# Two more products in seven steps: gate_w's second and w3's second product of the first group, with sums made by way of a PSUM bank

## The chip, the cores and the metric

The kernel runs on one NeuronCore of a Trainium2 chip. The metric is the device time of one launch in microseconds. Engines are named as the profile names them: PE is the matrix engine (PEld its weight loads), DVE the vector engine, ACT the scalar engine, POOL the GpSimd engine, SP the engine whose queue issues nearly all DMAs.

## What is computed

Inputs are 4,096 tokens of width 1,024, all in fp32. Cut to what matters, with the constants of the layers left out:

```python
xn = layernorm(u)                                  # 4096 x 1024
g = sigmoid(xn @ gate_w.T + gate_b); u_g = xn * g  # only its mean over time and 8 rows per block are used
s = c * scan(b * u_g) + (d + d_lr(mean(u_g))) * u_g
h1 = silu(xn @ w1.T)
h2 = silu(h1 @ w3.T)
h3 = h2 @ w2.T
out = scatter_add(gates * h3, top-2 of softmax(xn @ wr.T))   # into 8 rows
x = u + s * silu(out)
```

The scatter adds into the rows 0 to 7 alone, since the indices are those of the eight experts. Everything else of the output is a copy of u. The work is the product with gate_w (needed for 1,024 tokens), with w1 and w3 (needed for all tokens), and the routing.

## The kernel before, in words

The tokens are taken in four groups of 1,024 (`NS` = 4, `sb` 0 to 3). In each group there is a product `u` (xn with w1) and a product `m` (h1 with w3); group 0 has a product `g` (xn with gate_w) too. Each of these 1024 x 1024 x 1024 products is done by a scheme of the Strassen kind on two levels. The outer level has seven products of half size, numbered 1 to 7, of sums of the left blocks and sums of the weight blocks. The class `Half` (line 859) does one of them. Inside it, a second level of the same scheme makes seven steps of a half-size product instead of eight; a `plain` half has eight steps and needs no inner sums. A step (`small`, line 843) is four matmuls of 128x128 by 128x256.

An inner product needs four sums of each operand. `left_sums` (line 822) makes those of the left block and `fresh_sums` (line 559) those of a weight block, both on POOL, a quarter of a block (128x512) at a time, into tiles named `q`; `keep` also writes the weight sums to DRAM for the later groups. Where a half of group 0 is plain, `late_sums` (line 612) makes and keeps w3's sums at the beginning of group 1. Every partial result goes from PSUM to SBUF by an ACT copy or a DVE add (`first`, `more`): four times in a plain half, seven times in one with seven steps.

The outer sums of the left blocks are `s1` to `s4` (lines 777 to 820), each of four pieces of 128x512, on DVE in group 0. The outer sums of the weights are in `first_weights` (w1 and gate_w) and `first_w3` (`take`). Some of them go `with_bank` (line 599): ACT copies one operand to a PSUM bank and DVE takes the sum with that bank as its second operand. The banks are the accumulator `acc` (number 0), which is idle until the first scatter, and a bank `spare` (number 1). The gate's sigmoid (`gated`, line 1033) uses the same two.

The order of the work is written out. `line` lists the halves, `start` gives each a place; a half's steps stand two places apart, so two halves alternate, and one place is one step of PE. `at(place, f)` puts a piece of work at a place, and a generator's `yield n` puts its rest n places later. Each engine gets its instructions in the order that results, and keeps to it. The order within group 0 is u and g in turn (1, 2, 5, 6, 7, 4, 3), then m (1, 5, 6, 2, 7, 4, 3). `norm` (line 421) normalizes the next group's tokens during m: it loads rows of means and scales from DRAM, ACT copies them to the bank `spare`, and DVE subtracts and multiplies. Blocks (20), quarters (18) and the two X banks of PSUM are handed on in turn.

Of the kernel before, what the change touches and what calls it, by code (L numbers as in the profile page):

```python
# [14 lines left out]
ALU = mybir.AluOpType  # L15
# [7 lines left out]
def kernel(  # L23
# [162 lines left out]
    def at(place, f, *args):  # L186

        seq[0] += 1
        heapq.heappush(todo, (place, seq[0], f, args))
# [14 lines left out]

    order = {"u": (1, 2, 5, 6, 7, 4, 3), "m": (1, 5, 6, 2, 7, 4, 3)}
    line = []
    PLAIN_M = (2, 7)
    PLAIN_G = (1, 2)
    for i in order["u"]:
        line += [("u", 0, i, i == 1), ("g", 0, i, i in PLAIN_G)]  # L210
    line += [("m", 0, i, i in PLAIN_M) for i in order["m"]]
# [209 lines left out]
    def norm(sb, bcs):  # L421

        flat = bcs[sb].rearrange("(o s i t) p -> o s i (t p)", o=1, s=2, i=4)
        held = {}

        def load(n):
            held[n] = quarter()
            sync.dma_start(
                held[n].tile.rearrange("p (s n) -> p s n", s=2),
                flat[:, :, n, :].to_broadcast([P, 2, Q]),  # L430
            )

        load(0)
        for I in range(2):
            for a in range(2):
                n = 2 * I + a
                if n < 3:
                    load(n + 1)
                yield 1.5
                bc = ps_acc.tile([P, 2, Q], F32, tag="rows", name=f"bc_{sb}{n}")  # L440
                act.copy(bc.rearrange("p s n -> p (s n)"), held[n].tile)
                held[n].drop()
                for J in range(2):
                    p = part(xn[sb, I, J], a)
                    for s, op in ((0, ALU.add), (1, ALU.mult)):
                        yield norm_step[sb]
                        row = bc[:, s : s + 1, :].to_broadcast([P, 4, Q])
                        dve.tensor_tensor(p, p, row, op)

    norm_step = {1: 1.6, 2: 1.9, 3: 1.9}  # L450

    def route(sb):

# [123 lines left out]
    def sub(eng, out, p, q, n=4, step=0.5):  # L577

        for h in range(0, 4, 4 // n):
            eng.tensor_tensor(  # L580
                out[:, h : h + 4 // n], p[:, h : h + 4 // n], q[:, h : h + 4 // n], ALU.subtract
            )
            yield step

    free_banks = [0, 1]

    def spare_bank():


        while not free_banks:  # L590
            yield 0.25
        taken[0] = free_banks.pop(0)

    taken = [0]

    def bank_tile(n):
        return acc if n == 0 else ps_acc.tile([P, H], F32, tag="rows", name="spare")

    def with_bank(out, p, q, order=(0, 1, 2, 3), swap=False):


        for j in order:
            yield from spare_bank()
            n = taken[0]
            ps = bank_tile(n)
            act.copy(ps, q[:, j])
            yield 0.5
            a, b = (ps, p[:, j]) if swap else (p[:, j], ps)
            dve.tensor_tensor(out[:, j], a, b, ALU.subtract)
            free_banks.append(n)  # L610

    def late_sums(name, i):

# [100 lines left out]
    def first_w3():  # L714


        def S(i):
            return start["m", 0, i]

        b = {}  # L720

        def load(key, KN, uses):
            b[key] = load_w("w3", KN, uses)

        def take(i, p=None, q=None):

            if p is not None:
                yield from sub(pool if i in (7, 4) else dve, b[i], b[p], b[q], 4, 1)
                (b[p] if i == q else b[q]).drop()
                keep_block("w3", i, b[i])  # L730
            op_t["m", 0, i] = b[i]

        for place, i, KN, uses in (
            (S(1) - 28, 1, (0, 0), 3),
            (S(1) - 27, 5, (0, 1), 4),
            (S(1) - 20, 6, (1, 1), 5),
            (S(2) - 14, 2, (1, 0), 2),
            (S(2) - 8, 7, (0, 0), 3),
            (S(7) - 10, 4, (1, 0), 3),
            (S(3) - 14, 3, (1, 1), 2),  # L740
        ):
            at(place, load, i, KN, uses)
        at(S(1) - 22, take, 1)
        at(S(1) - 18, take, 5, 5, 1)
        at(S(1) - 10, take, 6, 6, 5)
        at(S(2) - 8, take, 2)
        at(S(2) - 2, take, 7, 6, 7)
        at(S(7) - 3, take, 4, 4, 6)
        at(S(3) - 8, take, 3)
        for i in order["m"]:  # L750
            if i in PLAIN_M:
                at(S(i) - 4, lambda i=i: op_t["m", 0, i].drop())
                continue
            at(
                S(i) + 2 - {1: 16, 5: 12, 6: 10}.get(i, 6),
                lambda i=i: fresh_sums("m", i, op_t["m", 0, i], True),
            )
# [16 lines left out]
    def s_engine(kind, sb):  # L774
        return pool if kind == "u" and sb > 0 else dve

    def s1(kind, sb, n):
        eng = s_engine(kind, sb)
        a21, a22 = left[kind, sb, (1, 0)], left[kind, sb, (1, 1)]
        o = block(1 + n)  # L780
        for q in (3, 0, 1, 2):
            eng.tensor_tensor(o[:, q], a21[:, q], a22[:, q], ALU.add)
            if q == 0:
                yield 0.5
        a21.drop()
        a22.drop()
        left[kind, sb, "s1"] = o

    def s2(kind, sb, n):
        eng = s_engine(kind, sb)  # L790
        p, a11 = left[kind, sb, "s1"], left[kind, sb, (0, 0)]
        o = block(2 * n)
        for q in (2, 3, 0, 1):
            eng.tensor_tensor(o[:, q], p[:, q], a11[:, q], ALU.subtract)
            if q == 3:
                yield 0.5
        p.drop()
        a11.drop()
        left[kind, sb, "s2"] = o

    def s4(kind, sb, n):

        eng = s_engine(kind, sb)
        o, a12 = left[kind, sb, "s2"], left[kind, sb, (0, 1)]
        for q in (2, 3, 0, 1):
            eng.tensor_tensor(o[:, q], a12[:, q], o[:, q], ALU.subtract)
            yield 0.5
        a12.drop()
        left[kind, sb, "s4"] = o

    def s3(kind, sb, n):
        eng = s_engine(kind, sb)
        a11, a21 = left[kind, sb, (0, 0)], left[kind, sb, (1, 0)]
        o = block(n)
        for q in (2, 3, 0, 1):
            eng.tensor_tensor(o[:, q], a11[:, q], a21[:, q], ALU.subtract)
            yield 0.5
        a11.drop()
        a21.drop()
        left[kind, sb, "s3"] = o  # L820

    def left_sums(kind, sb, i, n):
        a = left[kind, sb, S_OF[i]]
        s = []
        for j in range(4):
            o = quarter(n + (1, 1, 0, 0)[j])
            if j == 0:
                pool.tensor_tensor(o.tile, a[:, 2], a[:, 3], ALU.add)
            elif j == 1:
                pool.tensor_tensor(o.tile, s[0].tile, a[:, 0], ALU.subtract)  # L830
                s[0].drop()
            elif j == 2:
                pool.tensor_tensor(o.tile, a[:, 0], a[:, 2], ALU.subtract)
            else:
                pool.tensor_tensor(o.tile, a[:, 1], s[1].tile, ALU.subtract)
                s[1].drop()
            s.append(o)
            left_q[kind, sb, i, j] = o
            if j < 3:
                yield 2 * (A_AT[j + 1] - A_AT[j])  # L840
# [363 lines left out]
    for sb in range(NS):  # L1204
        n = 2 if sb == 0 else 1
        U = {i: start["u", sb, i] for i in range(1, 8)}
        at(U[5] - (12 if sb > 1 else 7), s1, "u", sb, n)
        at(U[5] - (9 if sb > 1 else 6), s2, "u", sb, n)
        at(U[7] - 10, s3, "u", sb, n)
        at(U[3] - (13 if sb == 0 else 8.6), s4, "u", sb, n)  # L1210
        if sb == 0:
            at(U[5] + 2, route, sb)
        M = {i: start["m", sb, i] for i in range(1, 8)}
        at(M[5] - 8, s1, "m", sb, 1)
        at(M[5] - 4, s2, "m", sb, 1)
        at(M[7] - 12, s3, "m", sb, 1)
        at(M[3] - 16, s4, "m", sb, 1)
        if sb > 0:
            for r in range(6 if sb < NS - 1 else 4):
                at(U[1] + 14 * r, copy_rows, 6 * (sb - 1) + r)  # L1220
        if sb + 1 < NS:
            bcs = {}
            at(M[1] - (46 if sb == 0 else 40), stats, sb + 1, bcs)
            for k, (I, J) in enumerate(HB):
                at(M[1] + (12 if sb == 0 else 4) + 3 * k, load_xn, sb + 1, I, J, USES[I, J])
            at(M[1] + (20 if sb == 0 else 8), norm, sb + 1, bcs)
            for IJ in HB:
                at(
                    M[1] + 26,
                    lambda sb=sb, IJ=IJ: left.__setitem__(  # L1230
                        ("u", sb + 1, IJ), xn[(sb + 1,) + IJ]
                    ),
                )
# [218 lines left out]
```

## Time and profile before

| | |
|---|---|
| median of three runs | 828.57 us (828.48 to 829.94) |
| profiled execution | 829.0 us, span 827.2 us |
| PE busy | 819.7 us, 99% of the span |
| DVE, POOL, ACT busy | 526.7, 483.8, 241.2 us |
| granted PE clock | 0.999 |
| DMA | 194.97 MB, mean 236 GB/s |

The profiled execution's time is 1.8 us over its span. All lines of the kernel are recorded through one helper (L89), so instructions are told apart by their tiles: `X_u<-q,q` is a matmul into a bank X of the product u, with a left sum and a weight sum as operands; `b` is a block, `q` a quarter. Durations of matmuls overlap each other. "Idle before" names what ended an engine's idle time just before an instruction.

### The profile page before, as it was taken

Reading aid. Unit: us, or ns where it says so; the run is one execution under the profiler, and the core shown is the slowest. Engines: PE = TensorE matmul, PEld = TensorE weight load, DVE = VectorE, ACT = ScalarE, POOL = GpSimd, SP = SyncE. Lnnn points to the kernel's source line nnn. Section 1 sums busy time; section 2 is a strip of 40 time slices with the busy share of each in tenths; the row PEclk is TensorE's granted clock in tenths of the full one; section 3 lists DMA queues with packets and bytes.
Section 4 is the critical chain, followed back from the end, with each engine's and each line's share of the span. In section 5 each row is a group of like instructions: output and inputs, shape, how many; then the busy total and the mean of one; then the engine's idle time right before and its main releaser. Section 6 shows DMA issues by size and latency. Waiting matters only on the chain.

```text
span 827.2 us, 11283 instructions
## 1 busy us (share of the span) xinstructions
PE 819.7 (99%) x4119; PEld 705.1 (85%) x4119; DVE 526.7 (64%) x875; ACT 241.2 (29%) x412; POOL 483.8 (58%) x378
## 2 busy tenths in 40 slices
PE   8999999999999999999999999999999999999997
PEld 7888888888888878888888788888888788888885
DVE  6976498878597523764996234765983246667643
ACT  1115216764022217442022147431122021220111
POOL 0379797866896759646446653853539454474300
PEclk9999999999999999999999999999999999999999
DMA  9946518542994979829956856659775555545700
GB/s 339 422 163 228 186 58 333 214 175 86 387 395 148 348 239 371 306 101 357 402 196 255 311 179 242 235 204 353 299 264 181 175 186 222 204 162 208 281 13 2
DMA packets 56215, 194.97 MB, mean 236 GB/s; under 512 B 6512, under 2 KB 9824, under 8 KB 44256
## 3 DMA queue, kind: packets, MB, share of 16 engines
q1 hardware_dynamic: 55840, 193.71, 63.3%
q8 instruction: 33, 0.54, 0.3%
q10 hardware_dynamic: 320, 0.54, 0.2%
q14 instruction: 22, 0.18, 0.1%
HBM read 171.10 MB, written 39.87 MB: 255 GB/s over the span
## 4 chain that ended last, share of the span: by engine, by line
PE 97%; DMA 1%; DVE 1%; SPq 0%; issue 0%; ACT 0%
PE X_m L89 23%; PE X_u L89 23%; PE Z_m L89 13%; PE Z_u L89 12%; PE Y_u L89 6%; PE X_g L89 6%; PE Y_m L89 5%; PE Z_g L89 4%; PE acc L89 2%; PE plT L89 2%; DMA b<-in_x 1%; PE Y_g L89 1%; SPq L89 0%; PE pp L89 0%; DVE bn L89 0%; PE bc L89 0%
## 5 line engine op out<-in xcount | busy, mean ns | idle before, releaser
L89 POOL TENSOR_TENSOR q<-b 128x512 f32<-128x512 f32 x144 | 195.7, 1373 | 213.7 <-PE X_m L89 53.9
L89 ACT ACTIVATE b<-b 128x512 f32<-128x512 f32 (+1 forms) x152 | 105.2, 696 | 330.3 <-DVE b L89 325.8
L89 DVE TENSOR_TENSOR b<-b,b 128x512 f32<-128x512 f32 x160 | 152.4, 970 | 3.1
L89 POOL TENSOR_TENSOR q<-b,q 128x512 f32<-128x512 f32 x91 | 127.4, 1403 | 15.8 <-issue 10.8
L89 POOL TENSOR_TENSOR b<-b,b 128x512 f32<-128x512 f32 x72 | 94.8, 1341 | 33.8 <-PE X_u L89 26.4
L89 PE MATMUL X_u<-q,q 128*128 128x256 f32 x432 | 102.4, 380 | 0.0
L89 DVE TENSOR_TENSOR b<-X_u,b 128x512 f32<-128x512 f32 x87 | 60.0, 690 | 61.1 <-PE X_u L89 60.5
L89 PE MATMUL X_m<-q,q 128*128 128x256 f32 x416 | 98.4, 379 | 0.0
L89 DVE TENSOR_TENSOR b<-X_m,b 128x512 f32<-128x512 f32 x84 | 57.5, 688 | 59.4 <-PE X_m L89 59.2
L89 POOL TENSOR_TENSOR q<-q,b 128x512 f32<-128x512 f32 x53 | 71.2, 1343 | 39.9 <-PE X_u L89 32.4
L89 PEld LDWEIGHTS X_u<-q,q 128*128 128x128 f32 x432 | 81.6, 190 | 12.3 <-issue 1.2
L89 PEld LDWEIGHTS X_m<-q,q 128*128 128x128 f32 x416 | 79.0, 190 | 11.5 <-issue 0.8
L89 DVE TENSOR_TENSOR b<-b,bc 128x1024 f32<-128x1024 f32 x56 | 67.6, 1212 | 4.2 <-ACT bc L89 4.0
L89 PE MATMUL X_m<-b,b 128*128 128x256 f32 x272 | 63.5, 379 | 0.0
L89 PE MATMUL X_u<-b,b 128*128 128x256 f32 x248 | 58.5, 379 | 0.0
L89 PEld LDWEIGHTS X_m<-b,b 128*128 128x128 f32 x272 | 51.4, 190 | 7.3 <-ACT b L89 0.3
L89 PEld LDWEIGHTS X_u<-b,b 128*128 128x128 f32 x248 | 47.0, 190 | 6.4
L89 PE MATMUL Y_u<-b,b 128*128 128x256 f32 x216 | 51.0, 379 | 0.0
L89 DVE TENSOR_TENSOR b<-Z_m,b 128x512 f32<-128x512 f32 x48 | 32.9, 687 | 28.5 <-PE Z_m L89 28.2
L89 PE MATMUL Z_u<-q,q 128*128 128x256 f32 x216 | 51.0, 379 | 0.0
L89 PE MATMUL X_u<-b,q 128*128 128x256 f32 x216 | 51.0, 379 | 0.0
L89 PE MATMUL Z_u<-q,b 128*128 128x256 f32 x216 | 51.0, 379 | 0.0
(168 smaller groups left out, 1150.4 us busy)
## 6 DMA issues: line engine op xcount, KB each, us to landing
q<-w SPq DMA_DIRECT2D x168, 256.0 KB, 3.7
b<-in_w SPq DMA_DIRECT2D x37, 1024.0 KB, 7.7
b<-w_T SPq DMA_DIRECT2D x25, 1024.0 KB, 6.8
b<-in_xT SPq DMA_DIRECT2D x15, 1024.0 KB
w<-q SPq DMA_DIRECT2D x56, 256.0 KB, 10.0
b<-in_x SPq DMA_DIRECT2D x12, 1024.0 KB
w_T<-b SPq DMA_DIRECT2D x8, 1024.0 KB, 4.3
b<-in_gw SPq DMA_DIRECT2D x6, 1024.0 KB, 14.2
```

The lines of the kernel that those rows point to most:

```text
L89: r = f(*args, **kwargs)
```

## The change

Gate_w's product 2 and, in group 0, w3's product 2 are no longer plain: they take seven steps and get inner sums on POOL. The late sums of w3's 2 in group 1 go. The outer sums s1 and s2 of u and s1 to s4 of m, in group 0, and w3's weight sums 5 and 6 are made by `with_bank`: u's with either bank, m's and w3's with the accumulator alone, one piece a place. `s1` of u comes two places earlier, `norm` starts earlier and waits four places after its first load, and its pieces in group 0 stand 1.85 places apart.

```diff
-    PLAIN_M = (2, 7)
-    PLAIN_G = (1, 2)
+    PLAIN_M = (7,)
+    PLAIN_G = (1,)
...
         load(0)
+        yield 4
         for I in range(2):
...
-    norm_step = {1: 1.6, 2: 1.9, 3: 1.9}
+    norm_step = {1: 1.85, 2: 1.9, 3: 1.9}
...
-    def spare_bank():
-        while not free_banks:
+    def spare_bank(of=(0, 1)):
+        while not any(n in free_banks for n in of):
             yield 0.25
-        taken[0] = free_banks.pop(0)
+        taken[0] = next(n for n in free_banks if n in of)
+        free_banks.remove(taken[0])
...
-    def with_bank(out, p, q, order=(0, 1, 2, 3), swap=False):
+    def with_bank(out, p, q, order=(0, 1, 2, 3), swap=False, op=ALU.subtract, of=(0, 1)):
         for j in order:
-            yield from spare_bank()
+            yield from spare_bank(of)
             n = taken[0]
             ps = bank_tile(n)
             act.copy(ps, q[:, j])
             yield 0.5
             a, b = (ps, p[:, j]) if swap else (p[:, j], ps)
-            dve.tensor_tensor(out[:, j], a, b, ALU.subtract)
+            dve.tensor_tensor(out[:, j], a, b, op)
             free_banks.append(n)
+            if of != (0, 1):
+                yield 0.5
...
-                yield from sub(pool if i in (7, 4) else dve, b[i], b[p], b[q], 4, 1)
+                if i in (7, 4):
+                    yield from sub(pool, b[i], b[p], b[q], 4, 1)
+                else:
+                    yield from with_bank(b[i], b[p], b[q], of=(0,))
...
+    BANKS = {("u", 0): (0, 1), ("m", 0): (0,)}
...
     def s1(kind, sb, n):
-        for q in (3, 0, 1, 2):
-            eng.tensor_tensor(o[:, q], a21[:, q], a22[:, q], ALU.add)
-            if q == 0:
-                yield 0.5
+        if (kind, sb) in BANKS:
+            yield from with_bank(o, a21, a22, (3, 0, 1, 2), op=ALU.add, of=BANKS[kind, sb])
+        else:
+            for q in (3, 0, 1, 2):
+                eng.tensor_tensor(o[:, q], a21[:, q], a22[:, q], ALU.add)
+                if q == 0:
+                    yield 0.5
...
     def s2(kind, sb, n):
+        while (kind, sb, "s1") not in left:
+            yield 0.25
+        if (kind, sb) in BANKS:
+            yield from with_bank(o, p, a11, (2, 3, 0, 1), of=BANKS[kind, sb])
...
     def s4(kind, sb, n):
+        while (kind, sb, "s2") not in left:
+            yield 0.25
+        if (kind, sb) == ("m", 0):
+            yield from with_bank(o, o, a12, (2, 3, 0, 1), True, of=BANKS[kind, sb])
...
     def s3(kind, sb, n):
+        if (kind, sb) == ("m", 0):
+            yield from with_bank(o, a11, a21, (2, 3, 0, 1), of=BANKS[kind, sb])
...
     def left_sums(kind, sb, i, n):
+        while (kind, sb, S_OF[i]) not in left:
+            yield 0.25
...
-        at(U[5] - (12 if sb > 1 else 7), s1, "u", sb, n)
+        at(U[5] - (12 if sb > 1 else 7 if sb else 9), s1, "u", sb, n)
...
-            at(M[1] + (20 if sb == 0 else 8), norm, sb + 1, bcs)
+            at(M[1] + (17 if sb == 0 else 4), norm, sb + 1, bcs)
```

## The prediction, made before the changed kernel ran

> **What bounds the kernel now.** I read the busy table first, then what the matrix engine waits for, then single steps of it, then the busy times of each stretch, and last the two engines that feed it around the change.
>
> ```profile
> PE 819.7 (99%) x4119; PEld 705.1 (85%) x4119; DVE 526.7 (64%) x875; ACT 241.2 (29%) x412; POOL 483.8 (58%) x378
> ```
>
> ```profile
> PE idle L89 <- POOL eps L89: 1.6, 1, 1.6
> PE acc L89 <- DVE q L89: 0.7, 1, 0.7
> PE mean L89 <- DVE q L89: 0.5, 1, 0.5
> PE pp L89 <- DVE accT L89: 0.3, 1, 0.3
> ```
>
> The second view is the whole list of PE's waits: 3.1 us, all in the first 20 us or at the very end. Nothing in the middle keeps PE from its next matmul, so the span is a sum of PE's steps. What a step costs is in PE's timeline (start, duration):
>
> ```profile
> 222.00 1.89 PE L89 MATMUL Y_m<-b,b 128*128 128x256 f32 x8
> 223.73 1.89 PE L89 MATMUL X_m<-b,b 128*128 128x256 f32 x8
> 225.46 1.89 PE L89 MATMUL X_m<-q,q 128*128 128x256 f32 x8
> ...
> 235.82 7.07 PE L89 MATMUL X_m<-b,b 128*128 128x256 f32 x32
> 242.72 7.07 PE L89 MATMUL Z_m<-b,b 128*128 128x256 f32 x32
> ```
>
> A step is four matmuls (eight records). From 223.73 to 242.72 lie 11 steps: 18.99 / 11 = 1.726 us each. The duration of 1.89 overlaps the next step; the distance of starts is the price.
>
> The feeding engines by stretch (stretch, then total, PE, PEld, DVE, ACT, POOL busy, clock, DMA share, GB/s):
>
> ```profile
> 17.00:66.00 49.00, 48.35 (x224) 41.98 (x223) 41.06 (x73) 9.52 (x18) 28.11 (x22) 1.00 0.69 277
> 190.00:212.00 22.00, 22.00 (x104) 19.29 (x103) 16.50 (x27) 10.74 (x18) 18.89 (x14) 1.00 0.30 105
> 212.00:255.00 43.00, 43.00 (x201) 37.86 (x200) 37.07 (x40) 7.42 (x11) 39.73 (x29) 1.00 1.00 395
> 255.00:276.00 21.00, 21.00 (x99) 18.47 (x99) 15.89 (x21) 4.27 (x7) 9.70 (x8) 1.00 0.39 126
> ```
>
> The first stretch holds gate_w's product 2, the next two w3's 1, 5, 6, 2, 7. In 212 to 255 POOL (92%) and DVE (86%) are almost full and DMA is full: there the change can go wrong. The granted clock is 1.00 throughout and can't move.
>
> **The change part by part.**
>
> *PE.* Gate_w's product 2 and w3's product 2 take 7 steps instead of 8; the built program has 2,059 matmuls for 2,067. Two steps at 1.726 are 3.45 us. A rule of the Trainium skill speaks against taking that at full value: "Perfetto Trace Analysis", section Identifying the Most-Contended Engine, says that matmul busy time is a bad measure of headroom and that LDWEIGHTS busy should be used. That is 85%, or 122 us in which PE would not be at its limit, and by it a removed step could vanish in gaps, or be worth only its weight loads: 2 x 8 x 190 ns = 3.0 us. The rows decide: starts stand 1.72 to 1.73 apart in every stretch I opened, and the list of waits has nothing there. I take 3.45.
>
> *DVE.* A 7-step product is evacuated seven times instead of four: 6 more of 0.69 us (`b<-X_u,b`, 687 ns). Against that, 32 block pieces (s1, s2 for u; s1 to s4 for m; w3's 5 and 6) leave the form b<-b,b (970 ns mean; 1041 up to 300 us) for one with an operand in PSUM, which the trace has at 0.69 (`b<-b,acc` at 65.80, 67.20, 68.97). So DVE has 6 x 0.69 - 32 x 0.28 = -4.8 us of work. None of it is on PE's path by itself.
>
> *ACT.* 32 copies more, 0.59 each (`COPY acc<-b`): 19 us on an engine that is busy 29%. They matter by order, not by load. The Trainium skill, "PSUM — Partial Sum Buffer", section Engine vs sequencer instructions, says that the queues of ScalarE and VectorE are strict FIFO: a DVE piece that waits for its copy holds every evacuation behind it, and a copy that waits for its bank holds the copies of X behind it. The trace shows it small: before the piece at 65.80 DVE idled 0.58 for `ACT acc`. By the rule, 32 x 0.58 = 18.6 us of DVE could be lost, a loss for PE wherever an evacuation has less spare than that; by the rows, only where the spare is short. I walked the new order, with the trace's durations, through both places, all times 1.73 earlier once gate_w's step is gone:
> - u, s1 and s2 (before at 52.93, 56.38, 60.59). First copy at 45.95 (acc, after the last normalization there), s1 complete at 55.8, where POOL, which waits for it, starts at 57.75 now; the silu table load (1.28) falls in the chain and is counted. s2 complete at 60.8. The tight evacuation is that of X_u's last step of product 2: matmuls end at 62.65, evacuated 63.4, and product 5 starts at 64.2 in the same bank. Spare 0.8, no stall.
> - m, one bank. Copies start at 188.9 (behind the last silu of h1), and are interleaved with sqrt, two table loads, and sigmoids of the gate. s1 complete at 196.5 (before: 192.97), s2 at 202.5. The copy of X_m product 1, second quarter, comes behind these at 197.9 to 198.5; PE wants its bank at 199.55: spare 1.1 (before: 1.7). First sum of product 5 on POOL 196.5 to 197.8, wanted at 201.3: spare 3.5 (before: 8.6). No stall.
> Cover: these spares. If they are gone, each us late is a us of PE.
>
> *POOL.* Four sums for gate_w's 2 and four left sums for w3's 2 are new; w3's four fresh sums come 60 us earlier than before. In the first place POOL starts waiting for nothing: it idled 4.46 us before 57.75. With four sums more it is done with product 5's right sides at 56.9 and s1 is there at 55.8, so it goes on 0.9 us sooner than now, on a PE that is 1.7 sooner; the first sum of product 5 ended at 61.2 for a use at 73.2. I take nothing. In the second place:
>
> ```profile
> 193.11 1.27 POOL L89 TENSOR_TENSOR q<-b 128x512 f32<-128x512 f32 x1 [12.87 <-ACT sd L89]
> ...
> 221.87 1.72 POOL L89 TENSOR_TENSOR q<-b,q 128x512 f32<-128x512 f32 x1
> ...
> 239.41 1.72 POOL L89 TENSOR_TENSOR q<-b 128x512 f32<-128x512 f32 x1
> ```
>
> 193.11 to 241.13 hold 32 operations, 48.0 us, of which 2.6 idle: 1.42 each; bounds are 1.23 (start to start undisturbed, 193.11 to 194.34) and 1.72 (while DVE does b<-b,b). In the new order the last sum of product 2 is the 31st from s1's end: 196.5 + 31 x 1.42 = 240.5. PE wants it 12 steps after the product's start: 222.0 + 12 x 1.726 = 242.7. Spare 2.2. By 1.23 it is 8.1; by 1.72, 249.8 and a stall of 7.1. I take 1.42 or less, since twelve of the b<-b,b that disturb it (s2, s3 and s4 of m) are bank forms then. Later products keep more than that, and POOL has 11 us free in 255 to 276.
>
> *SP and DMA.* Four writes w<-q (1.05 MB) move into the full stretch: at 395 GB/s 2.7 us for what is queued behind; one 1 MB load and four sums go from u's next group. What is loaded there is early: w3's 3 is issued at 233.28, lands 7.7 later by the median, and is used at 263.44. norm's first row load goes 3 steps earlier with its first copy kept in place; the copy at 229.45 came 6.62 late for that DMA, so this takes a block out of DVE. Its pieces spread from 1.6 to 1.85; the last is needed by s1 of the next group, at its own place, by POOL, which is far ahead of PE there (the first sum of that group's product 2 ends at 270.3 and is used at 291.1). For groups 2 and 3 only the load moves. I take 0; bounds -0.3 and +2.7.
>
> *Sum.* Profiled execution 829.0, span 827.2, so 1.8 around it. Span 827.2 - 3.45 = 823.75, time 825.55. The three runs' median is 828.57, 0.43 under the profiled one: 828.57 - 3.45 = 825.1.
>
> **The rivals.** A measurement of this kernel can't tell 0.2%, 1.66 us, from no change.
> 1. *Both steps are gained*: 825.1, with 824.4 to 825.9 for the spread of the runs and a stall under 0.8. Chance 0.62.
> 2. *The one-bank chain stalls PE.* The ACT/DVE ping-pong of m runs later than walked: half a us more at each of the four pieces of s1 makes 2, less the spare of 1.1, a stall of 0.9; one us each, 2.9. In u the same costs 1 or 2. Time 826 to 828.6. For it: strict order, table loads, one bank (and one wait of DVE for `ACT spare` at 76.21 was 1.55). Against: the others of that kind, from 65 to 72, were 0.49 and 0.58. Chance 0.23, half of it still faster by 0.2%.
> 3. *Slower: POOL becomes the bound in 212 to 255.* Decides at 1.49 us an operation (46.2 us / 31), where PE begins to wait; the gain is eaten at 1.60; at 1.66 it is slower by 0.2%. At 1.72 the stall is 7.1 and the time 832.2. For it: POOL at 92% and eight more operations. Against: 1.42 measured with more disturbance than will be left. Chance 0.12.
> 4. *The change doesn't do what it says*: the matmuls are gone from the program, and PE has no idle time to lose them in. 0.03, 828.6.
>
> **How the numbers follow.** Faster by over 0.2% (under 826.9): 0.62 + 0.12 = 0.74. Within: 0.11 + 0.03 = 0.14. Slower: 0.12. The time is case 1's. The range takes case 1 whole and case 2 to its end, 824.4 to 828.6; outside are case 3 and little else.
>
> **What would show it.** Right: the list of PE's waits unchanged, product 2 of gate_w and of w3 with x_q,q steps, X_u after plT as now but u's later steps 1.7 earlier, m's from product 7 on 3.45 earlier, span 823.8. Wrong: PE waiting for `ACT b` near 199 or 222 (case 2), for `POOL q` near 229 to 243 (case 3), or for DVE at 64 or 234. A clock under 1.00 would void the sum.

## The result, and the profile after

The change costs time. After it the kernel takes 843.02 us (median of four runs, 842.23 to 843.89) against 828.53 before: a ratio of 1.0172, 95% interval 1.0159 to 1.0185. The prediction was 825.1, with a range of 824.4 to 828.6. The two steps of PE are gained as forecast, and about 18 us are lost in one place that the forecast did not have.

The busy table and the clock row of the page after (the clock in tenths, a slice is 21 us):

```profile
PE 817.3 (97%) x4103; PEld 702.5 (84%) x4103; DVE 533.8 (64%) x881; ACT 258.6 (31%) x444; POOL 482.2 (57%) x386
...
PEclk9999999999969999999999999999999999999999
```

PE has 16 records fewer, the eight matmuls of two steps, and is busy 2.4 us less in a span that is 13.3 longer (840.5). One slice of the clock row has a 6. The list of PE's waits (us in total, times, longest) has one new line, and it is the first:

```profile
PE X_m L89 <- DVE b L89: 15.3, 1, 15.3
PE idle L89 <- POOL eps L89: 1.6, 1, 1.6
PE mean L89 <- DVE q L89: 1.3, 1, 1.3
```

It is one single wait, for a block from DVE. PE's timeline has its place (start, duration; a step costs the distance of the starts):

```profile
224.86 1.89 PE L89 MATMUL Z_m<-q,q 128*128 128x256 f32 x8
226.59 1.89 PE L89 MATMUL Z_m<-b,q 128*128 128x256 f32 x8
243.80 3.72 PE L89 MATMUL X_m<-q,q 128*128 128x256 f32 x8 [15.32 <-DVE b L89]
247.35 1.90 PE L89 MATMUL X_m<-q,b 128*128 128x256 f32 x8
249.09 1.89 PE L89 MATMUL Y_m<-b,b 128*128 128x256 f32 x8
```

At 243.80 the third step of w3's product 2 starts 17.21 after the step before it, not 1.73, and the step itself lasts to 247.35: 3.55. DVE's timeline tells what PE waited for:

```profile
221.61 0.69 DVE L89 TENSOR_TENSOR b<-Y_m,b 128x512 f32<-128x512 f32 x1 [0.77 <-PE Y_m L89]
222.34 20.72 DVE L89 TENSOR_TENSOR b<-b,b 128x512 f32<-128x512 f32 x1
242.98 1.28 DVE L89 TENSOR_TENSOR b<-X_m,b 128x512 f32<-128x512 f32 x2
```

One add, c12 = c22 + c21 in `whole` (product 6, first quarter), took 20.72 us, where the adds of this kind took 0.7 to 1.8 in the same stretch before the change. Both of its operands lie in SBUF. DVE keeps its order, so the evacuation of `X_m` behind it came at 242.98, and PE wanted that bank at 228.48. And POOL at that time:

```profile
220.48 1.27 POOL L89 TENSOR_TENSOR q<-b 128x512 f32<-128x512 f32 x1
221.71 1.26 POOL L89 TENSOR_TENSOR b<-b,b 128x512 f32<-128x512 f32 x1
222.94 1.26 POOL L89 TENSOR_TENSOR q<-b,q 128x512 f32<-128x512 f32 x1
...
241.25 1.25 POOL L89 TENSOR_TENSOR q<-b 128x512 f32<-128x512 f32 x1
254.98 1.28 POOL L89 TENSOR_TENSOR q<-b 128x512 f32<-128x512 f32 x1 [12.48 <-DVE b L89]
```

POOL runs from 195.78 to 242.50 with no gap over 0.08: 38 instructions, 1.23 from start to start. DVE's add became ready in the 22nd of them, waited through 16 more, and was done 0.56 after the last. Before the change, POOL's stream in the same stretch looked otherwise:

```profile
214.75 1.27 POOL L89 TENSOR_TENSOR b<-b,b 128x512 f32<-128x512 f32 x1 [1.30 <-DMA b<-in_w]
217.28 1.27 POOL L89 TENSOR_TENSOR q<-b 128x512 f32<-128x512 f32 x1 [1.27 <-DMA b<-in_w]
218.51 3.39 POOL L89 TENSOR_TENSOR b<-b,b 128x512 f32<-128x512 f32 x2
```

It had pauses of 1.30 and 1.27, and it met adds of DVE (218.51: two instructions in 3.39) again and again. A meeting, here and below, is a DVE instruction of two SBUF operands that is let in while POOL works. Pauses and meetings are both gone after: the added sums fill the pauses, and DVE's adds of s1 to s4 have become forms with a bank.

The windows give the price in clock (stretch and total, busy of PE, PEld, DVE, ACT, POOL, granted clock, DMA share, GB/s):

```profile
222.00:243.00 21.00, 6.48 (x31) 5.35 (x29) 20.97 (x3) 1.11 (x1) 20.50 (x17) 0.78 1.03 402
243.00:249.00 6.00, 5.20 (x16) 4.33 (x17) 5.57 (x9) 0.00 (x0) 0.00 (x0) 0.64 0.90 324
249.00:260.00 11.00, 11.00 (x53) 9.68 (x52) 10.51 (x14) 3.63 (x6) 5.02 (x4) 1.00 0.15 51
```

In 212 to 222 the clock was 1.00. In the six microseconds behind PE's pause it is 0.64 on average, and 0.50 within the first step (243.80 to 247.35), which costs 3.55 instead of 1.73. The sum: 825.1 as forecast, 15.3 of wait and 1.8 of slow clock are 842.2. The profiled execution took 842.23.

### The profile page after: what moved, and what is told of

It is laid out like the page before. It is cut to its first block, busy times and chain, and to the rows that moved or that the text cites. A ratio compares the mean times of both kernels' runs of the same rounds, so it can differ in the third digit from the quotient of the medians.

```text
span 840.5 us, 11293 instructions
## 1 busy us (share of the span) xinstructions
PE 817.3 (97%) x4103; PEld 702.5 (84%) x4103; DVE 533.8 (64%) x881; ACT 258.6 (31%) x444; POOL 482.2 (57%) x386
## 4 chain that ended last, share of the span: by engine, by line
PE 95%; DVE 3%; DMA 1%; issue 0%; SPq 0%; ACT 0%
PE X_m L89 23%; PE X_u L89 23%; PE Z_u L89 12%; PE Z_m L89 12%; PE Y_m L89 6%; PE Y_u L89 6%; PE X_g L89 6%; PE Z_g L89 3%; DVE b L89 3%; PE acc L89 2%; PE plT L89 2%; DMA b<-in_x 1%; PE Y_g L89 1%; PE pp L89 0%; DVE bn L89 0%; PE bc L89 0%
## 5 line engine op out<-in xcount | busy, mean ns | idle before, releaser
L89 DVE TENSOR_TENSOR b<-b,b 128x512 f32<-128x512 f32 x128 | 135.3, 1071 | 3.0
L89 POOL TENSOR_TENSOR b<-b,b 128x512 f32<-128x512 f32 x72 | 93.0, 1318 | 50.2 <-PE X_u L89 33.6
L89 PE MATMUL X_m<-q,q 128*128 128x256 f32 x432 | 104.0, 384 | 15.3 <-DVE b L89 15.3
L89 PEld LDWEIGHTS X_m<-q,q 128*128 128x128 f32 x432 | 83.0, 193 | 28.0 <-issue 16.5
L89 PE MATMUL X_m<-b,b 128*128 128x256 f32 x248 | 58.3, 379 | 0.0
L89 PEld LDWEIGHTS X_m<-b,b 128*128 128x128 f32 x248 | 46.9, 190 | 6.7 <-ACT b L89 0.3
L89 DVE TENSOR_TENSOR b<-Z_u,b 128x512 f32<-128x512 f32 x47 | 32.4, 690 | 30.6 <-PE Z_u L89 29.7
L89 PE MATMUL Y_m<-b,b 128*128 128x256 f32 x216 | 51.2, 380 | 0.0
L89 PE MATMUL Z_m<-b,q 128*128 128x256 f32 x216 | 51.1, 379 | 0.0
L89 PE MATMUL X_m<-q,b 128*128 128x256 f32 x216 | 51.0, 379 | 0.0
```

Source lines behind the costliest of these rows:

```text
L89: r = f(*args, **kwargs)
```

## The experiments

Theory A: the add was shut out by POOL. The rivals: B, it waited for something of its own (a DMA, a copy, the block that it writes); C, POOL is too slow for PE, the prediction's third case.

**Take away what can be shut out.** The adds of products 6 and 7 (c12, c22) go by way of the bank, like the change's own sums:

```diff
+    def by_bank(kind, sb, i, q):
+        c12, c21, c22 = (tiles[kind, sb, n] for n in ("c12", "c21", "c22"))
+        o = c12 if i == 6 else c22
+        yield from with_bank(o, c22, c21, (q,), op=ALU.add, of=(0,))
+        if i == 7:
+            done(kind, sb, 1, 1, q, c22)
...
-            dve.tensor_add(c12[:, q], c22[:, q], c21[:, q])
+            if k == ("m", 0):
+                at(here[0] + 0.25, by_bank, kind, sb, i, q)
+            else:
+                dve.tensor_add(c12[:, q], c22[:, q], c21[:, q])
```

(and c22's in the same way). In a second run only c12's go that way.

> The changed kernel, with the eight adds of w3's products 6 and 7 of the first group (c12 and c22, DVE, two SBUF operands) done as the change does its own sums: ACT copies one operand to the idle accumulator bank, DVE adds from there. Theory A (starvation: a DVE instruction with two SBUF operands cannot start while POOL streams without a gap, and waits until POOL itself has nothing ready): no DVE instruction of that kind is left beside POOL's stream, the 20.72 us add and PE's wait of 15.3 are gone, time 825 to 826. Theory B (the add waited for something of its own: a block, a DMA, a copy): the same stall at the add from the bank or at the next reader, 838 to 843. Theory C (POOL is too slow for PE): 832 or more, PE waiting for POOL q.

> As the other, but only the four adds of product 6 (c12) by the bank; those of product 7 (c22, the first some 10 us later) stay with two SBUF operands. A: the stall moves to the first c22 add, which starts to wait at 232 to 236 and ends when POOL's stream does, at about 242: 6 to 10 us of DVE, PE loses 4 to 9 of them, 829 to 835. If a stream of POOL also lets DVE in from time to time: 825 to 827. B: as before, 838 to 843.

With both: 825.27 us, ratio 0.9960 (0.9947 to 0.9974). PE's list of waits is that of before again:

```profile
PE idle L89 <- POOL eps L89: 1.6, 1, 1.6
PE acc L89 <- DVE q L89: 0.7, 1, 0.7
PE mean L89 <- DVE q L89: 0.6, 1, 0.6
PE pp L89 <- DVE accT L89: 0.3, 1, 0.3
```

Yet POOL is busy throughout 222 to 243, as the windows of the repetition (last run below) show:

```profile
222.00:243.00 21.00, 21.00 (x99) 18.49 (x98) 16.23 (x23) 8.27 (x13) 21.00 (x18) 1.00 1.03 405
```

So POOL isn't too slow for PE (against C), and the change's own one-bank chains cost PE nothing. With c12 alone: 834.51, ratio 1.0074 (1.0059 to 1.0089). DVE's timeline of that kernel, and then its list of PE's waits:

```profile
240.61 0.68 DVE L89 TENSOR_TENSOR b<-X_m,b 128x512 f32<-128x512 f32 x1
241.32 11.77 DVE L89 TENSOR_TENSOR b<-b,b 128x512 f32<-128x512 f32 x1
```

```profile
PE X_m L89 <- DVE b L89: 7.4, 1, 7.4
```

The stall has moved to the next add of two SBUF operands, c22's first: another instruction, 19 us later, which reads c22 and c21 like the first but writes another block. The sum c12 itself, from the same blocks into the same block, went without a stall once one operand lay in a bank. That speaks against B. The stall ends when POOL's stream does, which I had put at 242. The stream went on to 252.5 here; POOL's wait of 12.48 behind it, in the changed kernel for a block from DVE, is not there.

**One part of the change alone.**

```diff
-    PLAIN_M = (7,)
+    PLAIN_M = (2, 7)     # gate_w's part alone
...
-    PLAIN_G = (1,)
+    PLAIN_G = (1, 2)     # w3's part alone
```

> The changed kernel, but w3's product 2 plain again (8 steps, no sums of its own on POOL in the first group); gate_w's product 2 with 7 steps, bank sums and times as in the change. A: eight POOL instructions fewer up to 242, four of them in the stream ahead of 222 or behind it; POOL's stream ends sooner, so the add waits less: a stall of 15.3 less 4 to 8 times 1.23, that is 5 to 10, 832 to 838; none, and 826.8, if POOL pauses before 222. B: 838 to 843. C: 826.8, one step gained.

> The changed kernel, but gate_w's product 2 plain again (8 steps); w3's part as in the change. Theory A with the count (POOL lets no DVE instruction with two SBUF operands in once it has run some 15 instructions without a pause and without such a rival): POOL's stream around 196 to 242 is that of the change, so the add of about 20 us is there and PE waits about 15 us: 843 to 845, one step dearer than the change. If the four gate_w sums were what filled POOL's stream: no stall, 826.8.

Gate_w's part alone: 826.79, ratio 0.9979 (0.9970 to 0.9987), 1.72 below the 828.51 of before: one step at full price. This has all the bank forms of the change, and no stall. POOL's timeline, and then DVE's:

```profile
212.70 1.27 POOL L89 TENSOR_TENSOR b<-b,b 128x512 f32<-128x512 f32 x1 [0.68 <-DMA b<-in_w]
215.23 1.27 POOL L89 TENSOR_TENSOR q<-b 128x512 f32<-128x512 f32 x1 [1.26 <-PE Z_m L89]
```

```profile
222.44 0.76 DVE L89 TENSOR_TENSOR b<-b,b 128x512 f32<-128x512 f32 x1
```

Without w3's eight sums in this stretch (four left sums, four weight sums) POOL still pauses (0.68, 1.26), and the same add takes 0.76. No DVE add of two SBUF operands lies ahead of it in the stream: it became ready in POOL's 20th instruction from the start of the stream, but in the sixth from the last pause. So pauses alone are enough. My 5 to 10 us of stall were wrong; the clause "none if POOL pauses" was right. W3's part alone: 844.15, ratio 1.0193 (1.0175 to 1.0211), with the same wait of 15.3. The loss lies in w3's part.

**The meeting by itself.** These are kernels with nothing but streams of POOL instructions and one add of DVE that becomes ready in the middle. Cut to the core (an earlier DVE add, smaller instructions and copies are variants of it):

```python
def episode(k, n):
    pool.tensor_tensor(q[0], d, b1, ALU.subtract)      # behind the episode before
    for i in range(1, n):                              # n = k + 18
        pool.tensor_tensor(q[i], b0, b1, ALU.subtract)
    dve.tensor_tensor(f, ps, q[k], ALU.add)            # one operand in PSUM
    dve.tensor_tensor(d, f, b1, ALU.add)               # two in SBUF
```

> No part of the reference's computation: only streams of POOL subtractions (128x512, two SBUF operands, no wait between them) with one DVE add of two SBUF operands that becomes ready after POOL instruction k+1 of the stream (k = 1, 4, 8, 12, 16, 20, 24, 32), 17 more POOL instructions behind it. First eight with a DVE add from PSUM just ahead of it, then eight without, then three with an early DVE add at k = 1 too. Theory A in its simple form: every add waits for the end of its stream, about 20 us. A2 (what counts is how long POOL has run without a gap and without a rival): short waits, 0.6 to 1.8, at small k, about 20 us from some k between 14 and 22 on, and short again with the early add. B: 0.6 to 1.8 everywhere.

> No part of the reference's computation, streams of POOL again, each starting after a pause. In order: a DVE add from PSUM and then one of two SBUF operands that become ready after POOL instruction k+1, k = 9, 11, 12, 13, 14, 15, 16, 18; k = 10, 14, 16, 18 with an early DVE add behind the third POOL instruction; POOL instructions of half the size, k = 12, 16, 24, 32; an early add of 128x8 eight instructions ahead of k = 20 and 24; a DVE copy from SBUF instead of the add, k = 24; POOL copies (one SBUF operand) instead of subtractions, k = 24. 17 POOL instructions follow in each. A with the count: short waits up to some k between 10 and 15, some 20 us from there on; with an early add short at 10 and 14, where the count from it is 7 and 11, long at 18 if 15 is over the bound; half the size: by number the bound is at the same k, by time at twice; the tiny adds make the later one short. B: all short.

> Streams of POOL again (no part of the reference's computation), each after a pause, 17 instructions behind the add. In order: k = 13, 14, 13, 14, 13, 14; the add without the one from PSUM ahead of it, so that it is ready at the start of POOL's instruction k+2 and not in its middle, k = 12, 13, 14, 15; an early add of 128x64, 128x128, 128x256 and 128x512 behind instruction 10, then k = 18; POOL instructions of 128x256, k = 4, 6, 8, 10, then 6, 8, 10, 12 without the add from PSUM; of 128x128, k = 9, 11, 13. A with the count: 13 short and 14 long each time; the same bound or one more without the add ahead; the late add short behind an early one of 128x512 and long behind 128x64, the bound of size between; with the smaller instructions short up to the same number if it is a count, short everywhere here if it is a time (18 us, which k = 13 of 128x256 reaches nowhere).

`q[k]` is written by POOL's instruction k+1 of the episode, so the add of two SBUF operands, 0.72 later, becomes ready in the instruction k+2 where POOL's are of 128x512. In the first kernel k = 4 was long and k = 8 short, which a bound on k doesn't explain. The reason is that POOL had not paused ahead of k = 4: it came out of the episode before without a gap. Counted from POOL's last pause or meeting, everything fits. The second kernel, in which each stream starts after a pause, for k = 12, 13, 14, 15 (the add of two SBUF operands alone):

```profile
94.95 1.01 DVE L32 TENSOR_TENSOR d<-f,b 128x512 f32<-128x512 f32 x1
...
134.85 1.01 DVE L32 TENSOR_TENSOR d<-f,b 128x512 f32<-128x512 f32 x1
...
175.97 20.53 DVE L32 TENSOR_TENSOR d<-f,b 128x512 f32<-128x512 f32 x1
...
218.29 20.53 DVE L32 TENSOR_TENSOR d<-f,b 128x512 f32<-128x512 f32 x1
```

At k = 13 the add is ready in POOL's 15th instruction since the pause and is in after 1.01; at k = 14, in the 16th, it waits out the stream. In the third kernel the 15th went both ways (two long, two short). In all streams without an earlier meeting the 14th and earlier were short, the 16th and later long. What counts is a number of instructions and not a time. With POOL instructions of 128x256 (0.68 apart) the 14th was short (k = 12, no add ahead: 1.20) and the 15th long (k = 12 of the second kernel: 11.35). With 128x128 (0.41 apart):

```profile
763.66 1.02 DVE L32 TENSOR_TENSOR d<-f,b 128x512 f32<-128x512 f32 x1
...
778.48 6.78 DVE L32 TENSOR_TENSOR d<-f,b 128x512 f32<-128x512 f32 x1
```

These adds became ready at the turn from the 12th to the 13th and from the 14th to the 15th, 5.7 and 6.5 us into the stream; with 128x512 the bound lies at 18 us. In the whole kernel's traces, too (before, after and the nine variants of this section), every add of two full SBUF operands that became ready up to the 14th instruction since a pause or a meeting took less than 1.9, and the four that came later (the 22nd or the 37th) were shut out.

An earlier meeting starts the count again: with an add behind the third instruction, which delayed the fifth, k = 16 (the 18th, and 14th from there) was short, k = 18 (the 20th, 16th from there) long. How small may that meeting be? An add of 128x64, nine instructions ahead, was enough, though POOL's starts around it stay 1.22 apart. One of 128x8, let in during the 14th instruction and eight ahead in the second kernel, was not. In the next episode of that kernel the add of 128x8 itself became ready in the 18th, and was shut out for the whole rest of the stream:

```profile
630.96 1.21 DVE L32 TENSOR_TENSOR g<-q,b 128x8 f32<-128x8 f32 x1 [16.08 <-POOL q L32]
641.45 20.53 DVE L32 TENSOR_TENSOR d<-f,b 128x512 f32<-128x512 f32 x1
...
684.26 30.49 DVE L32 TENSOR_TENSOR g<-q,b 128x8 f32<-128x8 f32 x1 [20.96 <-POOL q L32]
```

A DVE copy from SBUF was shut out as well (20.27), and POOL copies with one SBUF operand shut the add out too (9.23, the rest of their stream). The adds from PSUM just ahead took 0.69 every time, also in POOL's 34th instruction.

**A meeting put into the changed kernel.** A DVE add that nobody needs, at the right moment:

```diff
+    def useless():
+        w = wr_sb.rearrange("p k g -> p (k g)").unsqueeze(1).to_broadcast([P, 2, Q])
+        o = quarter()
+        dve.tensor_tensor(o.tile.rearrange("p (a n) -> p a n", a=2), w, w, ALU.add)
+        o.drop()
...
+        if sb == 0:
+            at(M[1] + 14, useless)
```

> The changed kernel with one more DVE instruction that nobody needs, an add of two SBUF operands and full size (128x512), put behind the evacuation at 209.5, while POOL is in its 12th instruction of the stream. Theory A with the count: it is let in after 1.0 to 1.8 us and starts the count again, at 222 POOL stands at 10, the add there takes about 1 us: PE's wait of 15.3 is gone, 825 to 826. If what counts is only how far POOL is ahead: the useless add itself or the one at 222 waits for the end of the stream, 842 or more.

825.18 us, ratio 0.9968 (0.9958 to 0.9977). One instruction more, and the kernel is 17.8 us faster than without it. DVE's timeline:

```profile
210.06 1.11 DVE L89 TENSOR_TENSOR q<-wr_sb 128x512 f32<-128x512 f32 x1
...
222.26 1.63 DVE L89 TENSOR_TENSOR b<-b,b 128x512 f32<-128x512 f32 x1
```

The useless add is let in while POOL is in its 12th instruction; from the POOL instruction that it delays, the add at 222.26 comes in the tenth, and takes 1.63. POOL still has no pause there, and is as far ahead as before, in its 22nd instruction at 222: how far POOL is ahead isn't what shuts DVE out. Of its 22 executions four took 828.6 to 830.0, the others 824.6 to 825.7. Those four have no profile, and what they lost stays open.

Three adds of 128x8 (`scrap <- ones`) in place of the one:

> The changed kernel with three more DVE instructions, which nobody needs: adds of two SBUF operands, 128x8, at about 206, 212 and 218, while POOL streams. A with the count: each meets POOL after 8, 5 and 5 of its instructions and starts the count again; the add at 222 takes about 1 us, PE doesn't wait, 825 to 826. A without a count: the first of them is itself shut out until POOL pauses, a stall of over 30 us. If so small an instruction doesn't count as a meeting: 842 as the change.

842.51, ratio 1.0172 (1.0154 to 1.0190). They ran sooner than planned, at 198.3, 203.2 and 205.4, each in 1.0 to 1.3. The last is 13 POOL instructions ahead of the add, so this run alone proves little about their size. It agrees with the stream, which is one case: whether the size of the 128x8 or its place (the 14th instruction there, the 11th for 128x64) made the difference is not shown.

**The meetings that the change took away, put back.** h1's sums by two-operand adds again:

```diff
-    BANKS = {("u", 0): (0, 1), ("m", 0): (0,)}
+    BANKS = {("u", 0): (0, 1)}
```

(and the two tests for m in s3 and s4 go by `BANKS` too).

> The changed kernel, but the 16 pieces of h1's sums s1 to s4 in the first group are DVE adds of two SBUF operands again, as before the change; both products keep 7 steps, POOL keeps all its sums. A with the count: these pieces meet POOL at about 197 to 202 and 215 to 223 and each meeting starts the count again, so that no add is shut out: no PE wait, 825 to 826.5. A without a count (backlog alone shuts DVE out): a stall at the first such piece, over 840. C (POOL slowed to 1.72 by these meetings is too late for w3's product 2): 827 to 833, PE waiting for POOL q.

> The kernel with h1's sums on DVE again, once more: one of its five executions had taken 844.7, the others 824.7 to 825.3. Theory A: a shut-out of about 20 us in some executions, where POOL and DVE happen not to meet; 825 in the most. If the odd one was a disturbance from outside: 825 in all.

825.12 and 825.02, ratios 0.9958 (0.9941 to 0.9975) and 0.9957 (0.9944 to 0.9970). POOL does all the new sums, and it goes slower for it:

```profile
213.44 1.28 POOL L89 TENSOR_TENSOR q<-q,b 128x512 f32<-128x512 f32 x1
214.66 1.73 POOL L89 TENSOR_TENSOR b<-b,b 128x512 f32<-128x512 f32 x1
216.35 1.71 POOL L89 TENSOR_TENSOR q<-b 128x512 f32<-128x512 f32 x1
```

Every meeting costs POOL 0.45 (1.72 for 1.27) and DVE up to 1.1, and PE waits for neither. One of the ten executions took 844.66, which is what a shut-out would cost; it has no profile, and in the profiled ones POOL's count at a meeting is at most 11, where up to 14 was harmless. What happened there stays open.

**Versions that beat both.** Three are faster than the kernel before and after: the one with a useless add, the one with h1's sums on DVE, and the first, with no add of two SBUF operands left beside the long stream. The first has nothing left to be shut out there. It was run again:

> The version with c12's and c22's adds by the bank once more, which has no DVE instruction of two SBUF operands left beside POOL's long stream. Theory A: nothing is left to be shut out there, so every execution within 824.5 to 826.5, none near 843. If some executions go wrong for another reason (the kernel with h1's sums on DVE had one of ten at 844.7, the one with a useless add four of 22 at 828.6 to 830.0): some above 828 here too.

824.95 us, ratio 0.9956 (0.9942 to 0.9969), all five executions within 824.81 to 825.08.

## Why the prediction was wrong

- *PE, 3.45 us.* Right, and shown with the stall taken away: 828.51 - 825.27 = 3.24 and 828.53 - 824.95 = 3.58 in the two runs of the first version, 1.72 for gate_w's step alone. The rule of the Trainium skill that I set against it ("Perfetto Trace Analysis", section Identifying the Most-Contended Engine) would have given 3.0 or less by the prediction's estimate. The medians lie nearer to the distance of the starts, but the interval of the last ratio is 2.6 to 4.8 us, so the times alone don't exclude 3.0. The trace speaks for 3.45: without the stall PE's starts stand 1.73 apart through the whole stretch.
- *DVE.* Here it failed: "None of it is on PE's path by itself." This term was put at nothing, and one add in it cost DVE 20.0 us more, PE 15.3 of wait and 1.8 of slow clock. I had counted DVE's work, the spare of its evacuations and its waits for ACT, and had taken an add of two SBUF operands at 0.97 to 1.04, the mean of a group. In the group's mean there is no instruction that was shut out. Its price is 0.69 by itself, 1.0 to 1.8 where it meets POOL, and the rest of POOL's stream where POOL has gone 15 instructions without a pause or a meeting. (DVE's work fell more than the 4.8 that I said: 533.8 less the 20.0 of the shut-out is 513.8 against 526.7.)
- *POOL.* The same error from the other side: "I take 1.42 or less, since twelve of the b<-b,b that disturb it ... are bank forms then." POOL did get faster, 1.23; the 31st instruction ended at 233.96 where 240.5 was reckoned. I booked the missing disturbance as a gain. It was the thing that had let DVE in. Nor did I ask what becomes of "2.6 idle" once eight sums are put in: those pauses went too. Either the pauses (gate_w's part alone) or the meetings (h1's sums on DVE) are enough; the change took both away.
- *Case 3* had the right stretch and the right pair of engines, and the wrong victim: it let POOL be late for PE. POOL was early. Its worst time, 832.2, was far from 843. Among the signs of being wrong stood "for DVE at 64 or 234". PE's wait for DVE, 228.48 to 243.80, covers that place, but no case gave it a cause or a time.
- *Case 2 and ACT.* No stall from the chains, as walked. DVE's waits for `ACT acc` are 4.7 us in six, and for `ACT spare` 3.8 in five (before: 2.4 in three and 2.2 in two), and none of them reached PE; the sums of product 5 started at 195.78, walked at 196.5.
- *SP and DMA, u's part.* No wait of PE came from them.
- *The clock.* "Can't move" held only as long as PE did not pause. After 15.3 us it cost 1.8 more.

The Trainium skill has the rule that should have been weighed: "SBUF — State Buffer", section Who interferes with whom, says that a DVE instruction with two SBUF inputs contends with a GpSimd instruction that reads SBUF, and section SBUF: two separate sides says that whichever of the two starts first has the shared ports for its whole instruction, and the other is blocked. By that, I estimate that a meeting costs DVE at most one POOL instruction, 1.27 here. The runs agree up to the 14th instruction (at most 1.83, of which 0.69 is the add itself). Beyond it the add waited for the end of the POOL instruction that was running and then for 16 more, in the kernel as in the streams of 128x512, and the measurement decides.

## What to carry to other kernels

Where two engines contend for SBUF, look not only at what the meetings cost but at what lets the loser in. When a change fills POOL's pauses, or takes the rival instructions out of its stream, look for the first DVE instruction with two SBUF operands (or an SBUF copy) left in it, count POOL's instructions since its last pause or meeting, and put the rest of the stream as an upper bound on that one instruction. The cure is to give it an operand in PSUM, or to leave POOL a pause or a meeting within a dozen instructions. A group's mean says nothing of such a tail, and the change can make one where the profile of before has none.

## What was not expected of the hardware

- After 14 to 15 POOL instructions with neither a pause nor a meeting, DVE instructions that read two operands from SBUF, or copy from SBUF, are shut out until POOL pauses: 20.72 us in the kernel, 20.53 in the streams. Two pauses of 0.68 and 1.26 us were enough in the kernel; the shortest in the streams was 0.63, and a DVE add ran in it. The bound lies between the 14th and the 16th instruction for POOL instructions 1.22 us apart, between the 14th and the 15th at 0.68, and between the 12th and the 15th at 0.41. Why it is a number, and why that one, no run here shows.
- A meeting with an add of 128x64 starts the count again; in the one case tried in a stream an add of 128x8 didn't, though it was let in.
- After a pause of 15.3 us PE's next step took 3.55 instead of 1.73 (granted clock 0.50); after 7.4 us the next two took 4.99 instead of 3.45.
